# GNN message sums on column quarters: spans of 32 nodes, four at a time

## The chip, the core and the metric

The program runs on one core of a Trainium2 chip. A core has five engines that run side by side and meet at semaphores: TensorE (PE, matrix products into PSUM), VectorE (DVE), ScalarE (ACT), GpSimd (POOL, here mainly the issuer of gathers by index) and SyncE (SP, the issuer of plain DMAs). The metric is the device time of one execution in microseconds, the median of several runs. A profile is one further execution, whose own time is given beside it.

## What is computed

Four layers follow each other on 1250 nodes of 512 features: an attention over the edges of a graph, a mixture of 64 experts, a message passing with a gated update, and a small spline network. The graph has 21250 edges, sorted by their receiver `dst`, so a node receives 17 edges on the mean. The part around the change is the third layer:

```python
src, dst = (edge_index[0], edge_index[1])
m_in = jnp.concatenate([h[src], edge_attr], axis=1)
m = jax.nn.relu(m_in @ W1.T + b1) @ W2.T + b2
agg = jax.ops.segment_sum(m, dst, num_segments=h.shape[0])
gi = agg @ W_ih.T + b_ih
```

Each edge makes a message of 512 numbers from its sender's features and its own 128 attributes, and each node sums the messages of the edges that end in it. As `W2` is linear, the kernel sums the values after the relu and applies `W2` to the sums.

## The kernel before

Edges are stored in 167 tiles of 128 (`ET`), one edge in each partition. Before the stage, the node part of the first product, `h @ W1 + b1`, has been written for all nodes to a table in DRAM, `ptab`.

For each pair of tiles `messages` (L811) does this: POOL gathers the two tiles' rows of `ptab` by sender into `hg` (L817, recorded at the helper's line L195; four buffers of two tiles); PE multiplies the edge attributes `eat` with `w1e` into `pm` (L818, two PSUM buffers of two tiles); DVE adds the two into `m` (L820); ACT applies the relu in place (L821). `load_late` hangs the loads of later weights on some of these relus.

The loop of L829 goes over the tiles in groups of eight, 21 groups. A group is two windows of four tiles (`WT`), and each window has a fixed range of 64 nodes (`WN`) that is worked out from the window's number (`window`, L52), not from the data. One DMA brings `eat` for the group (L833). For each window DVE makes `at`, a matrix of zeros and ones that says for each edge which of the 64 nodes receives it (L838). Step `j` takes tile `j` of each of the two windows, and PE sums both: `at` as the weights, 64 columns wide, `m` as the moving data, with the first window's sums in PSUM partitions 0 to 63 and the second's in 64 to 127 of one tile `ps` (L847):

```python
for h, i in enumerate(js):
    nc.tensor.matmul(ps[h * WN:(h + 1) * WN], at[:, i], m[:, h], start=j == 0,
                     stop=j == WT - 1 or i == n - 1)
```

After four steps ACT copies `ps` to `s` (L850), PE transposes `s` in four pieces into `pt` (L861), and DVE adds the two windows' 64 columns into `rT`, the sums by feature, at the places of their nodes (L864). In three of the groups PE also turns `deg` into a row `cnt` (L855).

Edges whose receiver is further than 20 nodes from where its tile's number puts it (`SPREAD`, with `dnear` and `dres` made at the start) are counted in `far_i`. If the count is not zero, L867 runs a slow path for them. After it the gated update starts, with products of `w2` and `rT` (L949).

The order on each engine comes from the scheduler of the language. It starts from the order in which the program names the instructions, and may put a later one first if it is ready earlier. `tc.issue_after(x)` keeps the instructions of a block behind `x` on that engine. Waits between engines are made from the buffers.

The expert stage before it begins at L584 with work that depends on the routing: `order` (L617), the shared experts on three chunks of nodes (L619, L640, and L759 later), and the DMA `tokb` on SP (L622), which waits for the routing's scatters. The experts' weights follow on SP (L657).

Of the kernel before, what the change touches and what calls it, by code (L numbers as in the profile page):

```python
# [10 lines left out]
F32 = mybir.dt.float32  # L11
# [3 lines left out]
I32 = mybir.dt.int32  # L15
U32 = mybir.dt.uint32
AF = mybir.ActivationFunctionType
OP = mybir.AluOpType
AX = mybir.AxisListType
# [3 lines left out]
P = 128  # L23
N = 1250
NT = 10
NP = NT * P
LAST = N - (NT - 1) * P
D = 512
DC = D // P
E = 21250  # L30
ET = (E + P - 1) // P
# [10 lines left out]
CHUNKS = [(0, 512), (512, 512), (1024, 256)]  # L42
# [2 lines left out]
EPS = 1e-5  # L45
SPREAD = 20.0
HB = P // 2
WT, WN = 4, 64
NWIN = -(-ET // WT)


def window(w):  # L52

    return max(0, min(NP - WN, round((w + 0.5) * WT * P * N / E - WN / 2)))


def tiles_of(g):
# [17 lines left out]
def gnn_ffn_kernel(ctx: ExitStack, tc: tile.TileContext, a: dict, out: bass.AP):  # L75
    nc = tc.nc
# [15 lines left out]
    ident = const.tile([P, P], F32, name="ident")  # L92
# [37 lines left out]
        nc.vector.tensor_scalar(far_i, pf, -1.0, float(P * ET), op0=OP.mult, op1=OP.add)  # L130
    hT = const.tile([P, DC, NP], F32, name="hT")
    deg = const.tile([P, NT], F32, name="deg")

    def row(start, n):

# [448 lines left out]
    with tc.tile_pool(name="moe", bufs=1, side="right") as mw, tc.tile_pool(name="moe_w", bufs=4) as ew:  # L584
        with tc.tile_pool(name="moe_s", bufs=1) as keep, \
# [53 lines left out]
                                           op0=OP.add, op1=OP.add)  # L639
            shared_experts(*CHUNKS[2], keep, psum, psum1)  # L640

            loads, turn = [landed], cycle(accs)

            class Expert:
# [138 lines left out]
    with ExitStack() as kan:  # L783
        kw = kan.enter_context(tc.tile_pool(name="kan_w", bufs=1))
        with tc.tile_pool(name="gru_w", bufs=1) as gw:
# [22 lines left out]
            rT = gw.tile([P, DC, NP], F32, name="rT")  # L808
            nc.vector.memset(rT, 0.0)

            def messages(work, psum, parts, ahead, late=lambda i: None):  # L811

                k = len(parts)
                hg = work.tile([P, 2, D], F32, name="hg", bufs=ahead)
                pm = psum.tile([P, 2, D], F32, name="pm")
                for i, (t, eat_t) in enumerate(parts):
                    gather(hg[:, i], ptab, srci[:, t:t + 1])  # L817
                    nc.tensor.matmul(pm[:, i], eat_t, w1e, start=True, stop=True)  # L818
                m = work.tile([P, 2, D], F32, name="m")
                nc.vector.tensor_add(m[:, :k], pm[:, :k], hg[:, :k])  # L820
                with tc.issue_after(nc.scalar.activation(m[:, :k], m[:, :k], AF.Relu).ins):  # L821
                    late(parts[0][0])
                return m


            with tc.tile_pool(name="msg_e", bufs=3) as work, \
                    tc.tile_pool(name="msg_c", bufs=2) as chunks, \
                    tc.tile_pool(name="msg_ep", bufs=2, space=PSUM) as psum:
                for w in range(0, NWIN, 2):  # L829
                    t0 = w * WT  # L830
                    n = min(2 * WT, ET - t0)
                    eat = chunks.tile([P, 2 * WT * P], F32, name="eat")
                    nc.sync.dma_start(out=eat[:, :n * P], in_=a["edge"][:, t0 * P:(t0 + n) * P])  # L833
                    at = work.tile([P, 2 * WT, WN], F32, name="at", bufs=2)
                    for i in range(2):
                        ts = slice(i * WT, min((i + 1) * WT, n))
                        k = ts.stop - ts.start
                        nc.vector.scalar_tensor_tensor(  # L838
                            at[:, ts], iot[:, None, :WN].to_broadcast([P, k, WN]), float(window(w + i) + 1),
                            dnear[:, t0 + ts.start:t0 + ts.stop, None].to_broadcast([P, k, WN]),  # L840
                            op0=OP.add, op1=OP.is_equal)
                    ps = psum.tile([P, D], F32, name="ps", bufs=2)
                    for j in range(WT):
                        js = [i for i in (j, j + WT) if i < n]
                        m = messages(work, psum, [(t0 + i, eat[:, i * P:(i + 1) * P]) for i in js], 4, load_late)
                        for h, i in enumerate(js):
                            nc.tensor.matmul(ps[h * WN:(h + 1) * WN], at[:, i], m[:, h], start=j == 0,  # L847
                                             stop=j == WT - 1 or i == n - 1)
                    s = work.tile([P, D], F32, name="s", bufs=2)
                    nc.scalar.activation(s, ps, AF.Copy)  # L850
                    if w in (10, 12, 14):
                        c0, m = CHUNKS[w // 2 - 5]
                        pc = psum.tile([1, 512], F32, name="pt")
                        for j in range(m // P):
                            nc.tensor.matmul(pc[:, j * P:(j + 1) * P], deg[:, c0 // P + j:c0 // P + j + 1],  # L855
                                             ident, start=True, stop=True)
                        nc.scalar.activation(cnt[:, c0:c0 + m], pc[:, :m], AF.Copy)

                    pt = psum.tile([P, DC, P], F32, name="pt")
                    for c in range(DC):  # L860
                        nc.tensor.transpose(pt[:, c], s[:, c * P:(c + 1) * P], ident)  # L861
                    for i in range(2):
                        r = rT[:, :, window(w + i):window(w + i) + WN]
                        nc.vector.tensor_add(r, r, pt[:, :, i * WN:(i + 1) * WN])  # L864

            far = nc.values_load(far_i[:, :], min_val=0, max_val=P * ET)
            with tc.If(far):  # L867
                with tc.tile_pool(name="far_k", bufs=1) as keep, \
                        tc.tile_pool(name="far_w", bufs=2) as work, \
                        tc.tile_pool(name="far_q", bufs=2, space=PSUM) as psum:  # L870
                    sums = keep.tile([P, NT, D], F32, name="sums")
                    nc.vector.memset(sums, 0.0)
                    for t in range(ET):
                        eat = work.tile([P, P], F32, name="eatf")
                        nc.sync.dma_start(out=eat, in_=a["edge"][:, t * P:(t + 1) * P])
                        m = messages(work, psum, [(t, eat)], 2)[:, 0]
                        for j in range(NT):
                            at = work.tile([P, P], F32, name="at")
                            nc.vector.tensor_scalar(at, iot, float(j * P), dres[:, t:t + 1],
                                                    op0=OP.add, op1=OP.is_equal)  # L880
                            ps = psum.tile([P, D], F32, name="ps")
                            nc.tensor.matmul(ps, at, m, start=True, stop=True)
                            nc.vector.tensor_add(sums[:, j], sums[:, j], ps)
                    for j in range(NT):
                        pt = psum.tile([P, DC, P], F32, name="pt")
                        for c in range(DC):
                            nc.tensor.transpose(pt[:, c], sums[:, j, c * P:(c + 1) * P], ident)
                        rj = rT[:, :, j * P:(j + 1) * P]
                        nc.vector.tensor_add(rj, rj, pt)
# [335 lines left out]
```

## Time and profile before

| what | value |
|---|---|
| median of three runs | 2105.49 us (2105.23 to 2107.29) |
| the profiled execution | 2065.85 us |
| its span, first to last instruction | 2064.1 us |
| PE busy in the span | 1923.1 us, 93% |
| DVE, ACT, POOL busy | 50%, 36%, 22% |
| mean granted TensorE clock | 0.975 |
| first gather of the message stage (L195) | 1122.8 us |
| first product `pm` (L818) | 1125.4 us |
| last sum into `rT` (L864) ends | 1385.8 us |
| bytes moved from 1125 to 1386 us | 61.2 MB |

Times inside the span are in microseconds from its start. PE is the busiest engine in the whole and in most stretches. The message stage is about an eighth of the span, so its own stretch has to be looked at, not the shares of the whole. An f32 matmul appears in the profile as two PE instructions, each with a weight load (PEld) of its own, a transpose as one. In a row of groups the figures are the busy time, the mean length of one in ns, and the idle time of the engine just ahead of them with those who ended it.

### The profile page before, as it was taken

What the parts mean: (1) busy time and instruction counts of PE and PEld (TensorE: products, weight loads), DVE (VectorE), ACT (ScalarE), POOL (GpSimd) and SP (SyncE); (2) the same over time, 40 slices, a digit from 0 to 9 for tenths busy, and PEclk for the clock granted to TensorE, in tenths of its full rate; (3) what the DMA queues carried; (4) which work ended last, traced back from release to release, by engine and by line L of the source; (5) the groups of instructions that cost most, each with busy time, mean ns of one, the idle gap of its engine ahead of it and who ended that gap; (6) DMA issues with size and microseconds to landing.
All of it is one profiled execution on the core that took longest, in us unless ns stands there. A gap on an engine that the chain in (4) does not pass through costs nothing. (4 is left out here: it accounts for less than half of the span.)

```text
span 2064.1 us, 20996 instructions
## 1 busy us (share of the span) xinstructions
PE 1923.1 (93%) x7761; PEld 1030.8 (50%) x7761; DVE 1036.9 (50%) x1722; ACT 738.7 (36%) x1135; POOL 461.7 (22%) x435
## 2 busy tenths in 40 slices
PE   6999998789999999999998999989999968889889
PEld 4573233346666666666443333324444856456454
DVE  8666766732111111111163555541121389999995
ACT  3215653420111111111221343330112188777773
POOL 0000004071444444444301656630000000000000
PEclk9999999989999999999999999999999989999999
DMA  6000000204999999999843877740100020000000
GB/s 238 4 1 2 1 21 1 83 11 159 272 295 273 275 274 265 289 277 265 237 128 99 261 241 252 245 146 23 69 0 0 0 92 1 1 11 11 10 1 20
DMA packets 68947, 250.58 MB, mean 121 GB/s; under 512 B 11760, under 2 KB 14448, under 8 KB 59860
## 3 DMA queue, kind: packets, MB, share of 16 engines
q1 hardware_dynamic: 26914, 142.05, 19.3%
q0 software_dynamic: 36240, 92.89, 17.8%
q10 hardware_dynamic: 5666, 14.05, 2.0%
q8 instruction: 68, 1.11, 0.2%
q14 instruction: 59, 0.48, 0.1%
HBM read 211.98 MB, written 36.96 MB: 121 GB/s over the span
## 5 line engine op out<-in xcount | busy, mean ns | idle before, releaser
L195 POOL DMA_INDIRECT hg<-ptab,srci x167 | 158.0, 946 | 182.9 <-issue 120.6
L725 POOL DMA_INDIRECT acc<-y,goal x92 | 144.4, 1570 | 230.0 <-ACT y L723 106.6
L1088 PE MATMUL pk<-basis,w1s 128*128 128x256 f32 x640 | 156.3, 396 | 31.3 <-DVE basis L1070 31.3
L818 PE MATMUL pm<-w1e,eat 128*128 128x512 f32 x334 | 170.6, 626 | 6.6 <-DMA w1e<-in_W 6.6
L720 PE MATMUL py<-w,gT 128*128 128x512 f32 x368 | 169.5, 595 | 2.0 <-ACT gT L713 1.4
L1110 PE MATMUL py<-w2s,basis 128*128 128x512 f32 x320 | 147.7, 624 | 21.2 <-DVE basis L1070 21.2
L1088 PEld LDWEIGHTS pk<-basis,w1s 128*128 128x128 f32 x640 | 121.5, 196 | 67.1 <-DVE basis L1070 50.2
L820 DVE TENSOR_TENSOR m<-pm,hg 128x1024 f32<-128x1024 f32 x84 | 102.4, 1219 | 98.4 <-PE pm L818 96.1
L1047 DVE SCALAR_TENSOR_TENSOR cube<-held,knots,sq 128x512 f32<-128x512 f32 x180 | 137.0, 762 | 1.7 <-ACT sq L1043 1.7
L723 ACT ACTIVATE y<-py,gate 128x512 f32<-128x512 f32 (+1 forms) x92 | 63.3, 688 | 206.5 <-PE py L720 202.3
L473 DVE SCALAR_TENSOR_TENSOR wt<-ex,cnts 128x1024 f32<-128x1024 f32 (+1 forms) x120 | 119.5, 1040 | 28.4 <-ACT ex L471 28.1
L1043 ACT ACTIVATE sq<-held,negk 128x512 f32<-128x512 f32 x180 | 125.8, 709 | 20.6 <-DVE held L1035 20.6
L821 ACT ACTIVATE m<-m 128x1024 f32<-128x1024 f32 x84 | 88.2, 1050 | 124.4 <-DVE m L820 124.4
L471 ACT ACTIVATE ex<-ps 128x1024 f32<-128x1024 f32 (+1 forms) x120 | 101.1, 881 | 86.7 <-PE ps L466 65.2
L700 PE MATMUL pg<-w,xT 128*128 128x512 f32 x288 | 129.5, 592 | 0.2 <-issue 0.2
L1110 PEld LDWEIGHTS py<-w2s,basis 128*128 128x128 f32 x320 | 63.9, 201 | 103.0 <-issue 76.9
L195 POOL DMA_INDIRECT xg<-xtab,tok x92 | 90.0, 978 | 105.6 <-PE pt L696 57.9
L818 PEld LDWEIGHTS pm<-w1e,eat 128*128 128x128 f32 x334 | 56.3, 192 | 103.4 <-issue 98.2
L689 DVE TENSOR_TENSOR gT<-gx,pu 128x480 f32<-128x480 f32 x28 | 18.3, 655 | 177.0 <-PE pu L686 177.0
L720 PEld LDWEIGHTS py<-w,gT 128*128 128x128 f32 x368 | 65.6, 186 | 76.0 <-issue 71.9
L686 PE MATMUL pg<-xT,w 128*128 128x240 f32 x448 | 98.1, 372 | 2.9
L704 DVE TENSOR_TENSOR gs<-gs,pg 128x256 f32<-128x256 f32 x36 | 15.2, 421 | 168.6 <-ACT gs L703 168.6
(265 smaller groups left out, 3094.6 us busy)
## 6 DMA issues: line engine op xcount, KB each, us to landing
w<-in_experts SPq DMA_DIRECT2D x64, 1536.0 KB, 9.2
eat<-in_edge SPq DMA_DIRECT2D x20, 512.0 KB, 3.8
acc<-zero SPq DMA_DIRECT2D x22, 256.0 KB, 5.0
part<-acc SPq DMA_DIRECT2D x20, 256.0 KB, 4.2
w1s<-in_w1s ACTq DMA_DIRECT2D x4, 1024.0 KB, 4.9
w2s<-in_w2s SPq DMA_DIRECT2D x2, 2048.0 KB, 10.9
wih<-in_Wih ACTq DMA_DIRECT2D x4, 768.0 KB, 5.9
whh<-in_Whh ACTq DMA_DIRECT2D x4, 768.0 KB, 5.2
```

The source lines that it names most:

```text
L195: nc.gpsimd.indirect_dma_start(out=dst, out_offset=None, in_=table, in_offset=IndirectOffsetOnAxis(ap=at, axis=0))
L471: nc.scalar.activation(ex[:, :, :n], p[:, :, :n], AF.Exp, scale=DK ** -0.5)
L473: nc.vector.scalar_tensor_tensor(wt[:, :, :n], ex[:, :, :n], HUGE, cnts[:, b, None, n0:n0 + n].to_broadcast([P, 2, n]), op0=OP.min, op1=OP ...
L700: nc.tensor.matmul(ph[:m], xT[:, c, :m], self.w[:, c:2 * DC:DC], start=c == 0, stop=c == DC - 1)
L720: nc.tensor.matmul(py[:m], self.gT[:, f, at:at + m], self.w[:, k:k + 2].rearrange("p a b -> p (a b)"), start=f == 0, stop=f == 1)
L725: nc.gpsimd.indirect_dma_start(out=next(turn), out_offset=IndirectOffsetOnAxis(ap=goal[:m, self.r, h:h + 1], axis=0), in_=y[:m, j], in_off ...
L818: nc.tensor.matmul(pm[:, i], eat_t, w1e, start=True, stop=True)
L820: nc.vector.tensor_add(m[:, :k], pm[:, :k], hg[:, :k])
L1043: nc.scalar.activation(self.sq[k], self.x, AF.Square, bias=negk[:, k:k + 1])
L1047: nc.vector.scalar_tensor_tensor(self.cube[k], self.x, knots[:, k:k + 1], self.sq.pop(k), op0=OP.subtract, op1=OP.mult)
L1088: nc.tensor.matmul(pk[o], w[:, o * P:(o + 1) * P], b[:, c], start=half == 0 and g == 8 and c == 0, stop=half == 1 and g == 7 and c == 1)
L1110: nc.tensor.matmul(py[m], b[:, c, m * P:(m + 1) * P], w, start=g == 8 and c == 0, stop=g == 7 and c == 1)
```

## The change

A window is now two tiles (`WT` 2) with a span of 32 nodes (`WN`), and a group is four windows (`WG`), again eight tiles and 21 groups. The span of a window starts at the data's own first receiver of that window, no longer at a fixed node. In a step `j` four tiles, one of each window, are summed, the four windows' sums in PSUM partitions 0 to 31, 32 to 63, 64 to 95 and 96 to 127 of `ps`. There are two steps in a group. The four tiles of a step still come as two calls of `messages` of two tiles each.

As the four spans of a group begin where the data says, the sums cannot be added at fixed columns. In place of the transposes, PE multiplies the pieces of `s` with `to`, a 128x128 matrix of zeros and ones that brings each row of `ps` to its node's column in a fixed range of 128 nodes (`span`), and DVE adds all 128 columns into `rT` at once.

The sums of a step are issued one step later, behind the last product of the next step (`held`, `firsts` and `issue_after`), and the placing of a group behind the sums of its last step. `m` has four buffers instead of three, `at` and `to` have three.

What the new matrices need is worked out once, in the expert stage after L640: a DMA brings the receivers of each tile's first edge to all partitions (`head_i`), and some twenty DVE operations on up to 128x167 numbers make `inwin` (an edge's place in its span, or 0), `aim` (the node of each row of `ps`) and, with one small matmul, `out_i`, the count of edges outside their span or their 20 nodes. That count takes the place of `far_i` at the end of the stage; the slow path itself takes the same edges.

```diff
-WT, WN = 4, 64
-NWIN = -(-ET // WT)
+WT, WN, WG = 2, 32, 4
+NGRP = -(-ET // (WT * WG))
...
-def window(w):
-
-    return max(0, min(NP - WN, round((w + 0.5) * WT * P * N / E - WN / 2)))
+def span(g):
+
+    return max(0, min(NP - P, round((g + 0.5) * WT * WG * P * N / E - P / 2)))
...
+            head_i = keep.tile([P, ET], I32, name="head_i")
+            d0 = a["dst"]
+            nc.sync.dma_start(out=head_i,
+                              in_=bass.AP(tensor=d0.tensor, offset=d0.offset, ap=[[0, P], [1, ET]]))
+            head = keep.tile([P, NGRP, WG], F32, name="head")
+            nc.vector.tensor_copy(head.rearrange("p g q -> p (g q)"), head_i[:, ::WT])
...
+            nc.vector.memset(inwin, -1.0)
+            nc.vector.tensor_sub(inwin[:, :whole], dstf[:, :whole * WT].rearrange("p (w i) -> p w i", i=WT),
+                                 heads[:, :whole, None].to_broadcast([P, whole, WT]))
...
+            ok = keep.tile([P, ET], F32, name="ok")
+            nc.vector.tensor_scalar(ok, flat[:, :ET], 0.0, None, op0=OP.is_ge)
+            nc.vector.scalar_tensor_tensor(ok, flat[:, :ET], float(WN), ok, op0=OP.is_lt, op1=OP.mult)
+            nc.vector.scalar_tensor_tensor(ok, dnear, 0.0, ok, op0=OP.is_gt, op1=OP.mult)
+            nc.vector.scalar_tensor_tensor(flat[:, :ET], flat[:, :ET], 1.0, ok, op0=OP.add, op1=OP.mult)
+            inside = keep.tile([P, 1], F32, name="inside")
+            nc.vector.tensor_reduce(inside, ok, AX.X, OP.add)
+            po = psum.tile([1, 1], F32, name="pt", bufs=3)
+            nc.tensor.matmul(po, inside, ones[:, 0:1], start=True, stop=True)
+            nc.vector.tensor_scalar(out_i, po, -1.0, float(P * ET), op0=OP.mult, op1=OP.add)
+            nc.vector.tensor_scalar(aim, head[:, :, 0], qf, None, op0=OP.add)
+            for q in range(1, WG):
...
-                    nc.tensor.matmul(pm[:, i], eat_t, w1e, start=True, stop=True)
+                    firsts.append(nc.tensor.matmul(pm[:, i], eat_t, w1e, start=True, stop=True))
...
-                for w in range(0, NWIN, 2):
...
-                        for h, i in enumerate(js):
-                            nc.tensor.matmul(ps[h * WN:(h + 1) * WN], at[:, i], m[:, h], start=j == 0,
+                def summed(j, n, ps, at, sums):
+                    with tc.issue_after(firsts[-1].ins):
+                        for q, m in sums:
+                            i = q * WT + j
+                            nc.tensor.matmul(ps[q * WN:(q + 1) * WN], at[:, i], m, start=j == 0,
                                              stop=j == WT - 1 or i == n - 1)
+
+                def placed(g, ps, to):
+
                     s = work.tile([P, D], F32, name="s", bufs=2)
                     nc.scalar.activation(s, ps, AF.Copy)
...
                     pt = psum.tile([P, DC, P], F32, name="pt")
                     for c in range(DC):
-                        nc.tensor.transpose(pt[:, c], s[:, c * P:(c + 1) * P], ident)
-                    for i in range(2):
-                        r = rT[:, :, window(w + i):window(w + i) + WN]
-                        nc.vector.tensor_add(r, r, pt[:, :, i * WN:(i + 1) * WN])
...
+                        nc.tensor.matmul(pt[:, c], s[:, c * P:(c + 1) * P], to, start=True, stop=True)
+                    r = rT[:, :, span(g):span(g) + P]
+                    nc.vector.tensor_add(r, r, pt)
+
+                held = []
+                for g in range(NGRP):
...
+                    at = work.tile([P, WG * WT, WN], F32, name="at", bufs=3)
+                    nc.vector.scalar_tensor_tensor(
+                        at, iot[:, None, :WN].to_broadcast([P, WG * WT, WN]), 1.0,
+                        inwin[:, g * WG:(g + 1) * WG].rearrange("p w i -> p (w i)")[:, :, None].to_broadcast(
+                            [P, WG * WT, WN]), op0=OP.add, op1=OP.is_equal)
+                    to = work.tile([P, P], F32, name="to", bufs=3)
+                    nc.vector.tensor_scalar(to, iot, float(span(g)), aim[:, g:g + 1], op0=OP.add,
+                                            op1=OP.is_equal)
+                    ps = psum.tile([P, D], F32, name="ps", bufs=2)
+                    for j in range(WT):
+                        sums = []
+                        for q0 in range(0, WG, 2):
+                            qs = [q for q in (q0, q0 + 1) if q * WT + j < n]
+                            m = messages(work, psum, [(t0 + q * WT + j, eat[:, (q * WT + j) * P:][:, :P])
+                                                      for q in qs], 4, load_late)
+                            sums += [(q, m[:, i]) for i, q in enumerate(qs)]
+                        for todo in held:
+                            todo()
+                        held = [lambda g=g, j=j, n=n, ps=ps, at=at, sums=sums: summed(j, n, ps, at, sums)]
+                    held.append(lambda g=g, ps=ps, to=to: placed(g, ps, to))
+                for todo in held:
+                    todo()
...
-            far = nc.values_load(far_i[:, :], min_val=0, max_val=P * ET)
+            far = nc.values_load(out_i[:, :], min_val=0, max_val=P * ET)
```

## The prediction, made before the change was run

> **What bounds the kernel now.** I read three views in this order: busy time by stretch, the groups of the message stage (1125 to 1386 us of the span), then the timeline inside it.
>
> ```profile
> core 0: us, PE busy (x) PEld busy (x) DVE busy (x) ACT busy (x) POOL busy (x), PEclk, DMA share, GB/s
> 1150.00:1200.00 50.00, 50.00 (x157) 16.37 (x156) 28.73 (x64) 19.58 (x21) 31.32 (x34) 1.00 0.76 240
> 1250.00:1300.00 50.00, 50.00 (x150) 16.00 (x150) 25.94 (x33) 19.65 (x21) 31.42 (x34) 1.00 0.79 252
> ```
>
> PE has no idle time in the stage; DVE is at 52 to 57%, ACT at 39%, POOL at 63%, DMA at 0.76 to 0.79. The stage is PE's, and its length is the sum of what PE issues.
>
> ```profile
> L818 PE MATMUL pm<-w1e,eat 128*128 128x512 f32 x302 | 152.5, 618 | 0.0
> L195 POOL DMA_INDIRECT hg<-ptab,srci x146 | 138.0, 945 | 85.0 <-DVE m L820 59.8 <-issue 24.1 <-DVE negk L934 0.7
> L820 DVE TENSOR_TENSOR m<-pm,hg 128x1024 f32<-128x1024 f32 x76 | 92.6, 1218 | 88.8 <-PE pm L818 86.5 <-issue 0.7 <-ACT m L821 0.6
> L847 PE MATMUL ps<-m,at 128*64 128x512 f32 x310 | 83.7, 617 | 0.4 <-ACT m L821 0.4
> ```
>
> Groups of 1150 to 1480 us. PE waits for nobody; DVE's adds wait for PE (86.5 us) and POOL's gathers wait for DVE's release of their buffers (59.8 us). So POOL is held back by PE, and its own pace is what lies behind: 0.945 us plus 0.30 us of issue, 1.25 us for each gather.
>
> ```profile
> 1369.64 1.08 PE L847 MATMUL ps<-m,at 128*64 128x512 f32 x4
> 1370.65 1.98 PE L818 MATMUL pm<-w1e,eat 128*128 128x512 f32 x4
> 1372.57 1.08 PE L847 MATMUL ps<-m,at 128*64 128x512 f32 x4
> 1373.58 1.12 PE L818 MATMUL pm<-w1e,eat 128*128 128x512 f32 x2
> 1374.54 0.60 PE L861 MATMUL pt<-ident,s 128*128 128x128 f32 x4
> 1374.97 1.02 PE L818 MATMUL pm<-w1e,eat 128*128 128x512 f32 x2
> 1375.93 1.08 PE L847 MATMUL ps<-m,at 128*64 128x512 f32 x4
> ...
> 303.34 1.06 PE L485 MATMUL acc<-wt,V 128*32 128x512 f32 x8
> 304.23 1.04 PE L485 MATMUL acc<-wt,ones 128*32 128x512 f32 x8
> 305.20 1.14 PE L466 MATMUL ps<-QT,KT 32*128 32x512 f32 x8
> ...
> 482.39 0.63 PE L626 MATMUL pt<-moved,tokb 128*128 128x128 f32 x4
> 482.39 0.43 PEld L626 LDWEIGHTS pt<-moved,tokb 128*128 128x128 f32 x3 [0.23 <-issue]
> ```
>
> Timeline rows (start, length). I use distances between starts, since busy lengths overlap. Two tiles take 1372.57 - 1369.64 = 2.93 us: 1.92 for the products pm, 1.01 for the sums ps. In the shared experts 32 such instructions (L577) start at 468.66 and the next group at 482.39: 0.43 for one. Four are 1.72, so 0.20 of the 1.92 is a change of shape. Two half-column sums, if their halves run together, are 2 x 0.43 = 0.86, so 0.15 of the 1.01 is the change back: 0.35 for each alternation. The transposes add 3.36 - 2.93 = 0.43 once in eight tiles. The second block is the attention: L485 is exactly the shape that the sums will have (128 rows, 32 columns, 512 wide, four column quarters): eight instructions, four matmuls, in 0.89 us. The third is a real 128x128x128 matmul in f32: its weight loads come 0.143 us apart, two for a matmul.
>
> **What the Trainium skill says.** "TensorEngine Tiling (Array Packing)", Key Properties: tiles of the array run independently, but changing the tiling mode drains TensorE. The trace agrees with both: four quarters in 0.89 us, and 0.35 us for each alternation. "TensorE: Matmul & The Clock Gate", Part 3, gives 2.38 times for three 32-column tiles together; four quarters here do in 0.89 what four full-width matmuls do in 3.44 (3.9 times). The same page, Terms, says that transpose mode is four times faster for f32; in this trace a transpose is one instruction at 0.143 and a true matmul two, so giving it up doubles the count. "Perfetto Trace Analysis", Tensor Engine Instruction: the end of a TensorE instruction is estimated, which is why I count starts.
>
> **The change part by part.** All sums are against the profiled execution (2065.85 us, span 2064.1); the median of the runs shown is 2105.49, 1.019 times as long, and I scale the difference by that.
>
> Sums. Before: per eight tiles four alternations, each 0.86 of sums and 0.35 of change: 4.84 us. After: a step takes four tiles, one from each of four spans, so eight tiles need two blocks of eight instructions at 0.89 and two alternations: 2 x (0.89 + 0.35) = 2.48. Saved: 2.36 us. The stage has 167 / 8 = 20.9 such groups: -49.3 us. The change of shape was not measured between 128 and 32 columns; the step from quarters to rows in the attention (0.97 against 0.89) hints at 0.1 each way. I take 0.35, bounds 0.2 and 0.7: 42 x 0.15 = 6 us better to 42 x 0.35 = 15 us worse.
>
> Placing. The four transposes become true matmuls with the matrix `to`: eight instructions at 0.143 instead of four, 1.14 instead of 0.57; against the net 0.43 of before I take 1.1: +0.67 x 20.9 = +14 us. Bounds: +0.57 (12 us) and +1.0 (21 us). They need the copy s (0.60 us on ACT), which before is covered by one pm between 1373.58 and 1374.54. If that cover goes, 21 x (0.60 + some 0.5 of hand-over) = 23 us are lost. I expect it to stay: products of the next step are still there and need only free pm buffers.
>
> Products. Unchanged: 334 x 0.43 = 144 us. Their buffers stay at two; with a step of two pairs, pair k+2 needs the add of pair k, which has the other pair (1.72) or the sums block (1.24) and that pair to finish: 2.96 us against an add of 1.22. The sums held back by one step need a relu that ends 1.22 + 1.06 + about 0.4 after its products, while PE has a sums block and a whole step of products (4.7 us) before them. `m` has four buffers, two for each step; the step before last frees its own before they are needed. No new stall follows from these numbers.
>
> DVE, ACT. Per eight tiles: DVE four adds (4.88), one `at` (0.42 instead of two, as L838), `to` (0.28, as a 128x128 compare such as L609), one rT add of 128x512 (0.69 instead of two of 0.42): 6.3 of a group of about 10.5. ACT 4 x 1.05 + 0.60 = 4.8. Both hidden.
>
> POOL and DMA. The group on PE becomes 6.88 + 2.48 + 1.1 = 10.46 us, against 8 x 1.25 = 10.0 on POOL: still PE, by 4%. The floor that POOL sets: first gather at 1122.78, 167 x 1.25 = 209, landing 3.8 (median of these gathers), then about 6 us from the last add to the last rT: 1341 us, against 1386 before: at best -45. DMA moved 61.2 MB at a share of 0.74 on the mean of the stage; in a stage shorter by 14% that is 0.86, and some 0.92 while the late weights come (they are issued at the same tiles, so earlier). The expert stage runs at 0.95 with 277 GB/s, which would carry 61.2 MB in 221 us. Gathers may land later; the four `hg` buffers of two tiles give a gather some 6.5 us (10.46 less 2 x 1.25 of issue, 1.22 of add and hand-overs) before it holds anything up.
>
> Setup. About 23 DVE operations after the shared experts' last chunk: nine of 128x167 at about 0.3 us, fourteen small ones at 0.16: 5 us. DVE is busy 14.7 of 60 us between 440 and 500, and the shared experts run on PE there until 503; that hides them. `head_i` is one DMA on SP, behind tokb (issued at 464.08 when the route scatters have landed) and ahead of expert weights that PE needs at 505. If its landing is waited for by DVE ahead of an sT multiply, PE loses up to 4 us; at best 0. I take +1. The tiny matmul behind it: under 0.3. Start and tail of the stage: the last sums wait for the last relu as before, `pt` is longer by 0.6: +0.5, in the rounding.
>
> The fallback after the stage stays untaken: the receivers are sorted, and in the drawn edges the widest pair of tiles spans 18 nodes of 32.
>
> Sum: -49 + 14 + 1 = -34 us; scaled -35. 2105.5 - 35 = 2071.
>
> **The rivals.** (1) Gathers become late: with POOL at 96% and DMA near 0.9, products' adds wait for hg. For it: POOL's slack falls from 60 us to about 10, single landings of 13 us occur. Against: until 1145 us POOL ran at 1.25 us a gather and never waited for DVE. At 250 GB/s, about the most that the stage reached over 50 us, 61.2 MB take 245 us from 1122; with 6 us of tail and 1 of setup -12 is left: 2093. (2) The quarters don't run together here and cost as pairs: 2 x 1.72 a group; saved are two alternations (0.7) less placing (0.67): 0, 2105. L485 speaks against it. (3) Slower: the fixed order. Sums now sit behind the next step's products, so when such a product waits for its pm buffer PE can't take sums meanwhile, as it could before. If half of the 42 steps expose a whole add, relu and hand-over (2.7 us), 57 us are lost against 34 gained: +23, 2128. It decides from 34 / 42 = 0.8 us of wait a step; the 2.96 against 1.22 above speaks against it.
>
> **How the numbers follow.** Forecast 0.71 (its own range 2059 to 2082: POOL's floor, the change of shape at 0.7), rival 1 0.16, rival 2 0.05, rival 3 0.08. The range 2058 to 2095 takes in forecast and most of rival 1. A measurement of this kernel tells 0.2%, 4 us, from no change: faster 0.88, same 0.04, slower 0.08.
>
> **What would show it.** PE still without idle time and POOL above 90% busy with issue between 1150 and 1340; blocks of eight sums instructions with 32 columns, the next products about 1.0 us after their start; eight instructions for each placing in 1.1 us; the stage about 34 us shorter and all after it only shifted. Wrong if PE shows waits for adds or for s, or if a block of sums takes 1.7 us.

## The result, and the profile after

| what | kernel before | changed kernel |
|---|---|---|
| median of 20 runs each | 2104.91 us (2096.66 to 2110.16) | 2109.61 us (2105.66 to 2117.3) |
| ratio | | 1.0027, 95% interval 1.0015 to 1.0039 |
| profiled execution, span | 2065.85, 2064.1 us | 2107.03, 2105.3 us |
| first product to last placing (PE) | 259.2 us | 268.7 us |

The change makes the kernel 0.27% slower where I forecast 1.6% faster. The table's two profiles can't be subtracted, and this explains half of the puzzle: the experiments below fell on six chips, and the kernel before takes 2066 us on one of them (chip 6) and 2099 to 2101 us on the others (0, 4, 7, 8 and 15). By its time its profile above belongs to the first sort. Its timed runs, at 2105, and everything of the changed kernel in the table belong to the second. I call the sorts the 2066 chip and the 2100 chips.

Busy time by stretch, the changed kernel (busy us and instructions by engine, granted clock, DMA share, GB/s):

```profile
core 0: us, PE busy (x) PEld busy (x) DVE busy (x) ACT busy (x) POOL busy (x), PEclk, DMA share, GB/s
...
1160.00:1340.00 180.00, 159.31 (x568) 63.54 (x569) 89.26 (x134) 66.47 (x73) 109.66 (x117) 0.94 0.75 235
```

PE, which was busy without a break before, is busy 159 of 180 us, at a clock of 0.94. The groups of 1150 to 1480 us say who waits for whom:

```profile
L858 PE MATMUL pm<-w1e,eat 128*128 128x512 f32 x334 | 164.1, 631 | 27.7 <-DVE m L860 20.0 <-DMA w1e<-in_W 5.9 <-issue 1.8
L198 POOL DMA_INDIRECT hg<-ptab,srci x167 | 158.7, 951 | 193.1 <-issue 139.8 <-DVE m L860 51.8 <-DMA hg<-ptab,srci 0.9
...
L873 PE MATMUL ps<-m,at 128*32 128x512 f32 x334 | 53.2, 609 | 0.6 <-ACT m L861 0.6
...
L891 DVE TENSOR_TENSOR rT<-rT,pt 128x512 f32<-128x512 f32 x21 | 14.4, 687 | 50.6 <-PE pt L889 18.3 <-PE ps L873 17.2 <-PE pm L858 13.6
L879 ACT ACTIVATE s<-ps 128x512 f32<-128x512 f32 x21 | 12.4, 589 | 21.1 <-remote 18.2 <-PE ps L873 3.0
```

The sums are cheaper, as forecast: 53.2 us busy for 334 instructions of 32 columns, where 310 of 64 took 83.7. But PE now waits 20 us for DVE's adds, DVE waits 50.6 us ahead of 21 additions into `rT`, and the copy `s` waits for a "remote" that the profile can't name. The timeline of one of the gaps (start, length, engine, what):

```profile
1347.51 1.16 PE L889 MATMUL pt<-to,s 128*128 128x128 f32 x8
...
1349.10 1.22 DVE L860 TENSOR_TENSOR m<-pm,hg 128x1024 f32<-128x1024 f32 x1 [2.89 <-issue]
1350.36 1.06 ACT L861 ACTIVATE m<-m 128x1024 f32<-128x1024 f32 x1 [3.06 <-DVE m L860]
...
1352.27 0.95 POOL L198 DMA_INDIRECT hg<-ptab,srci  x1 [0.30 <-issue]
1353.22 1.07 PE L873 MATMUL ps<-m,at 128*32 128x512 f32 x8
1355.65 0.69 DVE L891 TENSOR_TENSOR rT<-rT,pt 128x512 f32<-128x512 f32 x1 [5.33 <-PE ps L873]
...
1356.45 2.35 DVE L860 TENSOR_TENSOR m<-pm,hg 128x1024 f32<-128x1024 f32 x2
1357.70 1.06 ACT L861 ACTIVATE m<-m 128x1024 f32<-128x1024 f32 x1 [6.29 <-DVE m L860]
1357.72 1.13 PE L858 MATMUL pm<-w1e,eat 128*128 128x512 f32 x2 [3.44 <-DVE m L860]
1357.94 0.95 POOL L198 DMA_INDIRECT hg<-ptab,srci  x1 [4.72 <-DVE m L860]
```

The placing ends on PE at about 1348.7; its addition on DVE, which needs nothing else, starts at 1355.65. It stands at the head of DVE's queue, so the adds behind it start at 1356.45 and the next products at 1357.72. PE's idle time is named "DVE m", but DVE was waiting for a completion of PE that was seven microseconds old. Meanwhile POOL issues gathers 1.25 us apart until 1353.22 and then stops, as its buffers come free only with the adds; the completion (the signal to the other engines that an instruction has ended) arrives 2.4 us after that. It is PE's completions that are late, not all of them: DVE's add ends at 1350.32, in the middle of that row of gathers, and its relu on ACT starts at 1350.36.

The names of the releasers have to be read with care here. On chip 6 the trace of the changed kernel holds 3851 updates of the semaphores of PE, DVE and ACT, where the instructions are marked to make 3845; on chip 0 it holds only 3660. Where a record is missing, the profile can name a wrong instruction, or none ("remote").

### The profile page after: what moved, and what is told of

It reads as the page before. It is cut to its first block, busy times and chain, and to the rows that moved or that the text cites. A ratio compares the mean times of both kernels' runs of the same rounds, so it can differ in the third digit from the quotient of the medians.

```text
span 2105.3 us, 21168 instructions
## 1 busy us (share of the span) xinstructions
PE 1912.4 (91%) x7847; PEld 1043.0 (50%) x7847; DVE 1031.7 (49%) x1724; ACT 740.3 (35%) x1135; POOL 461.2 (22%) x435
## 5 line engine op out<-in xcount | busy, mean ns | idle before, releaser
L858 PE MATMUL pm<-w1e,eat 128*128 128x512 f32 x334 | 164.1, 631 | 27.7 <-DVE m L860 20.0
L858 PEld LDWEIGHTS pm<-w1e,eat 128*128 128x128 f32 x334 | 62.0, 199 | 121.3 <-issue 89.9
```

The source lines that it names most:

```text
L858: firsts.append(nc.tensor.matmul(pm[:, i], eat_t, w1e, start=True, stop=True))
```

## The experiments

Three questions in turn: is the gain there at all, what takes it away, and does the same thing act elsewhere. Stage lengths are from the first `pm` to the last `pt` of the message stage on PE in the profiled execution. A gap is a distance of over 1.1 us between the starts of two matmuls that follow each other in the stage; the usual one is half a microsecond or less. Theory C, which several expectations name, says that PE's completions come late while POOL issues indirect DMAs without a pause. An indirect DMA is one that finds its rows by index, a gather or a scatter.

**Both kernels again, and the hold taken out, on the 2066 chip.** The first two are the kernel before and the changed kernel as they are. In the third each step's sums and placing are named at once:

```diff
-                        for todo in held:
-                            todo()
-                        held = [lambda g=g, j=j, n=n, ps=ps, at=at, sums=sums: summed(j, n, ps, at, sums)]
-                    held.append(lambda g=g, ps=ps, to=to: placed(g, ps, to))
+                        summed(j, n, ps, at, sums)
+                    placed(g, ps, to)
```

> The kernel before, unchanged, to see how it spends the 2105 us of its timed runs (its profile above took 2066). Theory A (the gap is not the change's): its timed executions have stretches in which TensorE's completions arrive late although nothing is waited for, as in the profile after (some 23 us between 343 and 366 us, in attention code that both kernels share); then this profile takes about 2105, with some 40 us of such stretches, part of them in the message stage, whose length would then be 275 to 300 us instead of 259. Theory B (the change brings the stalls): this profile is like the first one, 2066 us with a message stage of 259 us, or its extra 40 us lie wholly outside the message stage.

> The changed kernel, unchanged, a second execution. Theory A: about 2105 to 2115 us; the late completions lie at other places than in its first profile. Theory B: the nine gaps of 2 to 7 us in the message stage lie at the same places, because the order of the instructions makes them; the stage is 269 us again.

> The changed kernel with the sums and the placing issued at once, not one step later behind the next products. Theory B1 (the fixed order makes TensorE wait): the gaps in front of products and placings go and the kernel gains 20 to 30 us on the changed one. Theory A: within 8 us of the changed kernel, since the gaps are not made by the order; perhaps slower, as the sums now wait for the relu of their own step.

Measured: before 2064.39 us (ratio 0.9998, 0.9989 to 1.0007); changed 2032.39 us (0.9838, 0.9822 to 0.9854); without the hold 2069.77 us (1.002, 1.0014 to 1.0027). Stages 259.7, 229.3 and 267.1 us. The changed kernel there, PE's timeline and a stretch:

```profile
1251.11 1.06 PE L873 MATMUL ps<-m,at 128*32 128x512 f32 x8
1252.11 3.70 PE L858 MATMUL pm<-w1e,eat 128*128 128x512 f32 x8
1255.74 1.07 PE L873 MATMUL ps<-m,at 128*32 128x512 f32 x8
1256.73 3.70 PE L858 MATMUL pm<-w1e,eat 128*128 128x512 f32 x8
...
1269.01 1.05 PE L889 MATMUL pt<-to,s 128*128 128x128 f32 x8
1269.90 2.74 PE L858 MATMUL pm<-w1e,eat 128*128 128x512 f32 x6
```

```profile
1160.00:1340.00 180.00, 180.00 (x698) 72.14 (x698) 102.92 (x121) 81.51 (x88) 127.81 (x136) 1.00 0.85 280
```

Sums of four tiles are 1.0 us from the next products, the placing 0.89 us, PE has no idle time. The forecast of -34 us is -33.7 here. Without the hold, PE takes two quarters at a time, and each block costs as much as two half-column tiles cost before, 0.98 us:

```profile
1251.92 1.05 PE L873 MATMUL ps<-m,at 128*32 128x512 f32 x4
1252.90 1.12 PE L858 MATMUL pm<-w1e,eat 128*128 128x512 f32 x2
1253.95 1.05 PE L873 MATMUL ps<-m,at 128*32 128x512 f32 x4
1254.94 1.13 PE L858 MATMUL pm<-w1e,eat 128*128 128x512 f32 x2
```

So the gain needs all four quarters in one block: the hold is worth 37 us of these runs. No expectation of the three foresaw this chip: the changed kernel has none of the long gaps of its first profile here, and where theory B1 expected 20 to 30 us from taking the hold out, it costs 37.

**Both kernels on one 2100 chip (chip 0).**

> The kernel before, once more, so that both kernels have a trace from one and the same chip. If the chip is of the kind where the kernel before takes 2100 us or more: theory C (on such chips the completions of TensorE reach the other engines late while POOL issues indirect DMAs without a pause) expects a message stage of 258 to 265 us, as on the chip of 2066 us, since POOL pauses for VectorE in it, and the 35 to 40 us that this chip takes more all before the stage, in attention and routing. Rival (such a chip is slow in every stage alike, by its clock): the message stage longer by 2%, some 5 us, and the rest of the 40 us spread over all stages. On a chip of 2066 us it tells nothing new.

> The changed kernel, once more, on the same chip as the three other kernels of this call. On a chip of 2100 us or more, theory C: within 10 us of the kernel before (2100 to 2112 us), message stage 260 to 272 us, PE gaps of 2 to 7 us after runs of gathers at POOL's full pace. On a chip of 2066 us: 2032 us and a message stage of 229 us.

Measured: before 2099.16 us, changed 2101.34 us (1.0018, 1.0003 to 1.0032); stages 265.7 and 267.6 us. In the changed kernel the gaps are back: 14 of them, 31.6 us beyond a usual 0.52. The two kernels differ by 7.3 us in the spans of the profiled executions: +8.7 before the stage, +1.9 in it, -3.2 after. The first of these stands between attention and the first expert; it differs by up to 10 us among the kernels below, which have the same code there, and I did not settle it. How the kernel before issues its gathers on this chip:

```profile
1324.62 0.94 POOL L195 DMA_INDIRECT hg<-ptab,srci  x1 [1.17 <-DVE m L820]
1325.87 0.95 POOL L195 DMA_INDIRECT hg<-ptab,srci  x1 [0.30 <-issue]
1327.55 0.94 POOL L195 DMA_INDIRECT hg<-ptab,srci  x1 [0.73 <-DVE m L820]
1328.80 0.94 POOL L195 DMA_INDIRECT hg<-ptab,srci  x1 [0.30 <-issue]
```

Two gathers, then 0.42 us longer than POOL's own 0.30, because the buffer is not free. In the changed kernel PE is quicker, buffers are free in time, and POOL issues rows without a break, most of them of 12. These rows are what theory C blames. The kernel before has one such row too, while its buffers are empty at the start of the stage: some 16 gathers from 1148.3 to 1168.1. There, and nowhere else, it has a long gap, of 4.8 us until 1171.3; its copy `s` waits 6.1 us for a "remote". That is most of the 6 us by which its stage is longer than on chip 6. Distance from the end of the last placing matmul to its addition: on the 2066 chip a median of 0.04 us with 1 of 21 over 2 us; here 0.80 us, with 7 of 21 over 2 us and up to 6.86. (The one on the 2066 chip waits behind an add that waits for gathered rows.) The 84 relus on ACT, which wait for DVE, start at most 0.04 us after their add has ended or ACT is free, on either chip.

**More and fewer buffers for gathered rows, and a tidier order (chips 7 and 0).** The kernel before with 8 `hg` buffers for 4; the changed kernel with 3 for 4; the changed kernel with `placed` split so that the copy `s` comes a step before its matmuls, and the order on PE written out; and the last two together.

```diff
-                        m = messages(work, psum, [(t0 + i, eat[:, i * P:(i + 1) * P]) for i in js], 4, load_late)
+                        m = messages(work, psum, [(t0 + i, eat[:, i * P:(i + 1) * P]) for i in js], 8, load_late)
...
-                                                      for q in qs], 4, load_late)
+                                                      for q in qs], 3, load_late)
...
+                    with tc.issue_after(firsts[-1].ins):
+                        for c in range(DC):
+                            last = nc.tensor.matmul(pt[:, c], s[:, c * P:(c + 1) * P], to, start=True, stop=True)
+                    firsts.append(last)
...
+                    held.append(lambda g=g, ps=ps, to=to: ready.append((g, copied(ps), to)))
```

> The kernel before with eight gather buffers of two tiles in place of four, so that POOL issues its gathers one after the other for longer without waiting. Theory C (where the chip gives times of 2105, PE's completions come late while POOL issues indirect DMAs without a pause, as at 343 to 365 us of the profile after): on a chip where the kernel before takes about 2105 this one is slower than before by 10 us or more; on one where it takes about 2066 it is unchanged within 4 us, as PE bounds the stage. Rival (the late completions have to do with the new order or with the DMA share): unchanged within 4 us on either.

> The changed kernel with three gather buffers of two tiles instead of four, so that POOL waits for DVE's release in the message stage. Theory C: on a chip with before at 2105 it is faster than the 2110 of the changed kernel by 10 to 30 us; on one with before at 2066 it loses, as the gathers' landing (3.8 us) and add no longer fit into three pairs' time: 2035 to 2060. Rival: slower than the changed kernel on both.

> The changed kernel with the placing of a group held back by one more step and tied behind that step's products, with the sums behind it, so that no block of four sums is cut by a placing. In the second profile of the changed kernel one placing in two cuts a block: two instructions of sums took 0.98 us at 1260.36 and the other six 0.99. If those cuts cost as they look, some ten blocks of about 1 us are saved: 8 to 12 us faster than the changed kernel (2032), so 2020 to 2025 where before takes 2066. If PE is by now held by the gathers (POOL 1.25 us each, 209 us in sum), less than 4 us.

> The changed kernel with the placing held one step more, its matmuls put behind the products by hand, and three buffers for the gathered rows in place of four. On a chip of 2100 us or more, theory C: the buffers pace POOL a little, and the wait of ScalarE for the finished sums no longer stands ahead of the next relu: 2080 to 2092 us, faster than both kernels. Rival (three buffers only run dry): 2095 us or more. On a chip of 2066 us: 2025 to 2040 us; over 2040 us if three buffers are too few where no completion comes late.

Measured: 2114.81 us (1.0083, 1.0052 to 1.0114), 2090.31 us (0.9954, 0.994 to 0.9968), 2099.85 us (0.9998, 0.9979 to 1.0017) and 2088.66 us (0.9959, 0.9944 to 0.9973). With eight buffers the kernel before begins the stage with one row of 26 gathers until 1182.5 us, and its copy on ACT waits out that row:

```profile
1185.71 0.60 ACT L850 ACTIVATE s<-ps 128x512 f32<-128x512 f32 x1 [17.73 <-remote]
```

All sums had ended on PE at 1169.5, so the completion is 16.2 us late. PE has a gap of 16.4 us there and none over 2 us later, where nearly all rows are of two again. So the old code has the stall too when its rows are long. With three buffers the changed kernel is 10 us faster than the kernel before, its rows being shorter (most often of eight in the last of the four). Gaps of 27 us in sum are left, so this cures little. The order alone gains nothing that can be told from the kernel before; whether it gains the expected 8 to 12 us on the 2066 chip was not run.

**Half the gathers off POOL (chip 0, where both kernels ran as they are).** The second tile of each pair is filled by a plain DMA of the same size on SP's queue. This leaves out the true rows of half the edges.

```diff
-                    gather(hg[:, i], ptab, srci[:, t:t + 1])
+                    if i:
+                        nc.sync.dma_start(out=hg[:, i], in_=ptab[:P])
+                    else:
+                        gather(hg[:, i], ptab, srci[:, t:t + 1])
```

> The changed kernel with the second tile of every pair filled by a plain DMA of the same size on SP's queue (the first 128 rows of the table, so the gathered rows of half the edges are left out; bytes and buffers stay). POOL issues half the indirect DMAs and has pauses of over 1 us between them. On a chip of 2100 us or more, theory C: no PE gaps over 1.5 us in the message stage, stage near 230 us, time 2065 to 2075 us. Rival (the share of the DMA engines, 0.85, delays the completions): the gaps stay, stage 255 to 270 us, time 2095 to 2112 us. Rival B (the order of PE's queue makes the gaps): gaps stay too. On a chip of 2066 us: stage 225 to 232 us, no difference from the changed kernel.

Measured: 2059.77 us (0.9826, 0.978 to 0.9872), below what theory C expected, stage 227.0 us, no gap but two of up to 1.3 us at its very end. The same stretch in the changed kernel on this chip, and here:

```profile
1160.00:1340.00 180.00, 157.28 (x567) 62.68 (x567) 88.76 (x134) 66.02 (x72) 108.80 (x115) 0.95 0.74 234
```

```profile
1160.00:1340.00 180.00, 180.00 (x690) 71.54 (x692) 105.46 (x148) 80.32 (x88) 63.73 (x69) 1.00 0.83 284
```

The DMA engines are busier (0.83 against 0.74) and PE is full, so it is not their share that delays the completions, and not the order of PE's queue. It goes with the indirect DMAs that POOL issues; whether with POOL's own work on them or with what carries them out, this run doesn't separate. The stage nearly adds up as well: 227.0, 30.2 of gaps (31.6 less the two at the end, which this run has too) and 8.6 (half of 17.1 us in which the record of the clock has it at 0.5) make 265.8, against 267.6 measured. "TensorE: Matmul & The Clock Gate" of the Trainium skill, Part 1, says that idleness sets the gate to half and that some 3.4 us of work release it; here 3.4 or 6.8 us at half clock begin near the end of four gaps, of 3.2 to 6.2 us. In the first profile of the changed kernel a gap of 2.5 us has it too and one of 3.3 has not, so these runs give no sharp limit.

**Breaking the rows without a wait (chips 4 and 15).** A fill of a small tile on POOL, which nobody reads, behind each pair of gathers: 128, 256 and 480 columns. And, as a rival, an order that bears late completions: copy, placing and addition each held a step longer, with buffers that wait for their own last reader only ("tolerant").

```diff
+                with tc.issue_after(got.ins):
+                    nc.gpsimd.memset(blank, 0.0)
...
+                        while put:
+                            added(*put.pop(0))
+                        while ready:
+                            put.append(placed(*ready.pop(0)))
+                        while done:
+                            g0, ps0, to0 = done.pop(0)
+                            ready.append((g0, copied(ps0), to0))
```

> The changed kernel with a fill of a small tile (128x128, 0.2 us on POOL at the program's start) on POOL behind each pair of gathers, which nobody reads. It breaks up the rows of gathers without a wait for another engine. On a chip of 2100 us or more, theory C1 (any break in POOL's rows of gathers lets TensorE's completions through): gaps gone, message stage 228 to 245 us, 2060 to 2080 us. Theory C2 (only pauses of about 1 us or more do, as in the kernel before): gaps stay, stage 260 to 275 us, 2095 to 2110 us. On a chip of 2066 us: stage 228 to 240 us, POOL's own length (167 gathers of 1.25 us and 84 fills of 0.2 to 0.5 us, 226 to 251 us) being what sets it if above TensorE's 225.

> The changed kernel with the copy of finished sums, the placing and its addition on VectorE each held one step (5 us) longer, and buffers whose waits are for their own last reader only. Nothing is paced. If late completions cost time only because the copy on ScalarE and the addition on VectorE wait at the head of their queues, with the next messages behind them (theory D), this takes most of the gaps away on a chip of 2100 us or more: stage 230 to 245 us, 2060 to 2080 us. If the completions of the products themselves come late too (theory C as it stands), gaps stay: stage 250 to 265 us, 2085 to 2105 us. On a chip of 2066 us: 2025 to 2035 us.

> Both edits in one. On a chip of 2100 us or more: not slower than the better of the two by more than 5 us; 2060 to 2075 us if either theory C1 or D holds, over 2090 us if neither. On a chip of 2066 us: 2025 to 2045 us.

> As the run with the short fill, whose 0.22 us were for the most part hidden in the 0.30 us that POOL leaves between two gathers in any case (pairs 2.58 us apart in place of 2.50), but with a fill of 256 columns: some 0.35 us, pairs about 2.71 us apart, a break of 0.2 us. On a chip of 2100 us or more: if a break of 0.2 us is enough, no gaps, stage 228 to 240 us, 2060 to 2075 us; if not, gaps as before, stage 258 to 272 us, 2090 to 2105 us. On a chip of 2066 us: stage 229 to 236 us, 2030 to 2042 us.

> The same with a fill of 480 columns: some 0.57 us, pairs about 2.93 us apart, a break of 0.42 us behind each pair, as the kernel before has it from its wait for VectorE. Theory C (unbroken rows of gathers hold TensorE's completions back, and the kernel before is spared since its rows are of two): on a chip of 2100 us or more no gaps over 2 us from row ends; POOL's length, 83.5 pairs of 2.93 us, sets the stage, 245 to 252 us, 2075 to 2090 us. Rival (the break must be a wait, or what matters is how far the gathers run ahead): gaps of 2 to 7 us stay, stage over 258 us, 2095 us or more. On a chip of 2066 us: stage 245 to 250 us, 2046 to 2055 us, slower than the changed kernel there.

> The same fill of 480 columns in the kernel with the longer holds. On a chip of 2100 us or more within 6 us of the run before it if theory C holds, since POOL sets the pace in both; if gaps stay there, this has fewer of them and is 5 to 10 us faster.

| kernel | true break behind a pair | stage | time | ratio (95% interval) |
|---|---|---|---|---|
| fill 128 | 0.08 us | 268.6 us | 2100.99 us | 0.9999 (0.9986 to 1.0013) |
| fill 256 | 0.18 us | 263.2 us | 2095.44 us | 0.9985 (0.9973 to 0.9997) |
| fill 480 | 0.37 us | 254.1 us | 2084.77 us | 0.9924 (0.9901 to 0.9947) |
| tolerant | none | 265.4 us | 2095.72 us | 0.9977 (0.9961 to 0.9993) |
| tolerant, fill 128 | 0.08 us | 262.3 us | 2093.34 us | 0.9958 (0.9936 to 0.9979) |
| tolerant, fill 480 | 0.37 us | 246.0 us | 2088.01 us | 0.9939 (0.9914 to 0.9964) |

A fill costs POOL less than its length, as part of it lies in the 0.30 us that POOL leaves anyway. With the largest:

```profile
1284.50 0.95 POOL L198 DMA_INDIRECT hg<-ptab,srci  x1 [0.30 <-issue]
1285.45 0.51 POOL L861 MEMSET blank<- 128x480 f32 x1
1286.12 0.95 POOL L198 DMA_INDIRECT hg<-ptab,srci  x1 [0.16 <-issue]
```

The dose answers: the longer the break, the less time in gaps, though POOL does more. With no break (chip 0) and with breaks of 0.08 (chip 4), 0.18 and 0.37 us (chip 15) the gaps make 31.6, 30.4, 25.9 and 18.8 us beyond the usual distance, and 10, 7, 7 and 3 of them are over 2 us. "Any break is enough" (C1) falls, and so does "only about 1 us is" (C2). At 0.37 us the cure is partial: a gap of 6.1 us and one of 3.1 are left where theory C expected none over 2. Of the many small ones part is POOL's own pace, 83.5 pairs of 2.87 us or 240 us; how much, these runs don't tell. The last row's stage is that of its profiled execution, 2080.84 us, one of the fast ones of its five; its time can't be told from that of the fill alone. The tolerant order alone leaves the stage at 265.4 us, so it isn't just two instructions in a bad place: the gaps move to where the adds wait for the products themselves.

**The same rows elsewhere (chip 8).** Both kernels issue the route's scatters (`tokt`, L451 of the changed kernel) in rows of 24, 24 and 12 beside attention and the first shared experts. The fill of 480 columns goes behind each pair of these, once together with the gathers' fills and once alone.

```diff
+                    if k % 2:
+                        with tc.issue_after(s.ins):
+                            nc.gpsimd.memset(rest, 0.0)
```

> The changed kernel with the fill of 480 columns behind each pair of gathers in the message stage, and the same fill behind each pair of the route's scatters (tokt), which both kernels issue in unbroken rows of 24, 24 and 12 while attention and shared experts run. On a chip of 2100 us or more, theory C says that these rows cost the 35 to 40 us that such a chip takes more before the stage: attention then ends near 408 to 418 us in place of 428, and the time is 2045 to 2070 us, faster than with the gathers' fills alone (2085 us). Rival (that extra time has another cause): attention still ends near 428 us, 2080 to 2095 us. On a chip of 2066 us: 2045 to 2060 us.

> The changed kernel with the fills behind the route's scatters alone; the message stage is as changed, with unbroken rows. On a chip of 2100 us or more, theory C: attention ends near 408 to 418 us, and the message stage keeps its gaps at 262 to 272 us: 2070 to 2095 us. Rival: 2100 to 2115 us. On a chip of 2066 us: 2032 to 2040 us, the fills being hidden there.

Measured: 2060.76 us (0.9819, 0.9801 to 0.9837) and 2078.66 us (0.991, 0.9893 to 0.9927). The last attention matmul starts at 406.9 and 406.1 us, against 427.6 in both kernels on chip 0 and 405.7 on the 2066 chip. A softmax of the routing waits for sixteen small matmuls of PE; first in the changed kernel on chip 0, where they end at about 456.8 and POOL goes on with scatters and two plain DMAs until 466.4 us, then with both fills, where they end at 436.0:

```profile
468.45 0.29 DVE L397 TENSOR_TENSOR pr<-ps,rb 128x128 f32<-128x128 f32 x1 [17.98 <-remote]
```

```profile
436.04 0.29 DVE L397 TENSOR_TENSOR pr<-ps,rb 128x128 f32<-128x128 f32 x1 [6.34 <-PE ps L394]
```

With the scatters' fills alone the message stage stays at 267.6 us, with both it is 250.4: the two losses are one thing in two places, and they add. The kernel with both fills beats the kernel before by 38.5 us on this 2100 chip. It was not run on the 2066 chip, nor was the kernel before run with the scatters' fills, so how much of its lead the change itself would keep is open: by these runs the scatters' fills are worth about 22 us (from the changed kernel on chip 0 to this chip) and the gathers' about 18 (on this chip).

## Why the prediction was wrong

- What bounds the stage (PE's issue), the sums (-49) and the covered copy `s`: right on the 2066 chip. That its -33.7 us fall on the forecast -34 is in part luck: in the spans they are -2.4 before the stage, -30.4 in it, where -35 were forecast, and -1.8 after it.
- The placing (+14) was a little too cheap. Alone it takes 0.89 us where 1.1 was assumed, but of 20 placings there 6 stand inside a block of sums, which then costs 0.98 and 0.99 us in place of 1.00: by the distances of starts, about +17 in all. At the stage's start PE also waits some 3 us for adds that wait for gathered rows.
- The 0.35 us for an alternation held: a step without placing takes 4.62 us (1252.11 to 1256.73), where 8 x 0.43 + 0.89 + 0.35 = 4.68 were expected.
- Setup +1: on the 2066 chip the stage starts 2.4 us earlier, so it costs nothing there. On chip 0 it starts 8.7 us later; not settled, see above.
- The step that failed is "POOL and DMA": "The group on PE becomes 10.46 us, against 8 x 1.25 = 10.0 on POOL: still PE, by 4%", together with "No new stall follows from these numbers" under the products. I asked whether the gathers come in time and took it as free that POOL runs at its full pace. On the 2100 chips it isn't: in rows of gathers without a break PE's completions reach DVE and ACT up to 7 us late. The term is +30.2 us of gaps and +8.6 of half clock on a stage of 227, and was zero in my sum. POOL's 60 us of waiting, which I read as slack that could be spent, were what kept the kernel before out of this, but for the one row at its start.
- Rival 1 was nearest (POOL's lost slack), but for another reason: DVE waits only 7.4 us for gathered rows in the first profile of the changed kernel, as far as the records tell, and a higher DMA share with half the gathers cured it. Rival 2 fell on the 2066 chip. Rival 3 gave the right symptom, products that wait for their `pm` buffer ahead of sums, but its price was worked out from adds and relus in time, and on the 2066 chip no step exposes one.
- A sign was there, though not of the cause. The trace and the times of before differed by 40 us, and I put that into a factor of 1.019. All stages alike was an assumption: on chip 0 the stage after the messages takes the same time as on chip 6, and attention and routing take most of the rest.

What stays open: why chips differ, and what in POOL's issue holds a completion back. The runs show when it arrives: of the ten gaps over 2 us of the changed kernel on chip 0, six end their wait 2.2 to 2.3 us after the end of a row's last gather, one after 2.9 us, and three within 0.7 us of a gather's end.

One rival stands untested, that the recording itself has a part in it. Only the traces of the 2100 chips lack semaphore updates, and no run is known to have been made without recording. Against it as the whole cause: the run with both fills lacks as many (3641 are left of 3846), though it has 17 us of gaps in place of 31.6.

## What to carry to other kernels

An engine's slack can be what another one lives on: before a change takes an engine's pauses away, ask what passes in them, completions included. A check that one engine stays busier than another, here PE by 4%, doesn't ask that. When an instruction waits for one that ended microseconds ago, and the profile says "remote", look at what POOL was issuing. If a profile and the timed runs of the same kernel disagree by more than the change is worth, find out in which stage before scaling.

## What the runs showed of the hardware

- On five of the six chips used for the experiments PE's completions came late beside unbroken rows of indirect DMAs on POOL (1.25 us apart): by up to 7.0 us at 12 in a row, and 16.2 us at 26. DVE's completions to ACT did not (0.04 us at most). Beside rows of two with 0.42 us between PE's did not either, nor on chip 6 beside rows of 12 and one of 26.
- A fill of 128x128 on POOL behind an indirect DMA takes 0.22 us and adds 0.08; one of 128x480 takes 0.51 and adds 0.37.
- A POOL row's bar is not its transfer. "Perfetto Trace Analysis" of the Trainium skill, DMA Instruction — SWDGE (GPSIMD), says that the bar ends when the descriptors are made; here the bar is 0.95 us, and gathers on the 2066 chip land 3.3 to 7.7 us after their start.
- Two quarters of columns at a time (four instructions) cost 0.98 us from block to products, four quarters (eight) 0.99.
